# Two convolution layers with attention: where the second layer queues the next convolution's inputs and loads the third image

## The chip, the cores and the metric

The kernel runs on one core of a Trainium2 chip. The metric is the device time of one execution in microseconds (us); the time before is the median of three runs. One further execution was recorded by the hardware profiler, and all durations below come from it.

The engines are TensorE (PE in the profile, with its weight loads as PEld), VectorE (DVE), ScalarE (ACT), GpSimd (POOL) and SyncE (SP). Each works through its own queue in order. SyncE and ScalarE also issue DMAs from their queues: an issue that has to wait holds up what stands behind it.

## The reference, cut to what matters

Four images of 512 channels x 32 x 32 go through two layers. Each layer normalises its input by groups of 16 channels and adds its own result to the input. The first layer is a selective state-space scan and isn't touched. The second is, for each image:

```python
x_top    = conv1x1(x, w_top)                # 64 channels
x_center = conv1x1(x, w_center)             # 64 channels
x_bottom = conv3x3(x, w_bottom)             # 512 channels
sp  = softmax over all of (x_center^T x_top)   # 1024 x 1024, one softmax for the whole map
x   = x + (sp @ x_bottom)                   # reshaped as the image
out = conv3x3(x, w_out)
result = input + out                        # x above is the normalised input
```

All is float32.

## The kernel before

**The second layer's steps for image b.** The functions stand below with the profile's line numbers.

- norm loads the image (x1t, eight loads of 256 KB on ScalarE's queue, L1285), takes its statistics on VectorE (bn_stats, L1292, L1293), averages them by groups with a small matmul (pm_l, L1299), does the same for the deviations (pv_l, L1303), takes the root on ScalarE (L255, L256, with two table loads) and writes the normalised image xg (L1306). padded allots xg and clears its border with four memsets on POOL (L232 to L235).
- scores does the two 1 x 1 convolutions (pt, L1324), which ScalarE turns into center (L1329) and top (L1336), and the score map in 16 pieces (psc, L1345). ScalarE copies each piece into a tile st (L1349); eight such tiles, tag "st", hold the map. VectorE takes a maximum of each (mx, L1350), and ScalarE the exponential in place (L1359).
- conv3 named b0 to b3 is the 3 x 3 convolution with w_bottom, and conv3 named o0 to o3 the one with w_out. It works in transformed form: six row positions p, taken in the pairs (1, 2), (3, 4), (0, 5), times four column positions q, each a product of 4 x 4 chunks (m_b or m_o, L1494, 192 matmuls in a convolution). Its inputs are made by first_inputs or inputs: ScalarE and POOL make e and f (L1393, L1394), or POOL makes g, h, k, l; VectorE sums them into rr (L1396, L1397, L1460, L1469); and spread makes the four v from rr (L1374 to L1377). Each (p, q) needs 1 MB of transformed weights (uw_b, uw_o, L1490), which SyncE loads into three buffers of tag "u". ScalarE (L1502) and VectorE (L1510) take the products out of five PSUM buffers.
- attend multiplies the scores with the convolution's result, in eight steps k of 16 matmuls (pat, L1546), and adds each to xg on VectorE (L1559): I call this the attention's sum, and k = 7 the last one. The result of pat is in one of three PSUM buffers of tag "ps", which pt, psc, pm_l, pv_l and the final transposes use as well. For the first two images attend also does the remaining transforms of w_out, in pieces (wt, wr, wo, L1408 to L1437): VectorE computes them, SyncE stores them to u_o. wt, wo and the weights uw share the three "u" buffers, and rr and wr share the one of tag "rr".
- finish turns the result back with 32 transposes (po, L1586), adds it to the input loaded as o (L1576, L1591) and stores it (L1601, ScalarE's queue). last does it for the last image.

**The order.** The images go in pairs (a = 0 and a = 2). In a pair: b(a), attention of a with the norm of a + 1 inside, scores of a + 1, b(a + 1), inputs of o(a), attention of a + 1, o(a), finish, o(a + 1), finish. The norm of the third image (a + 2) is called inside o(a + 1), after its first inputs, through the argument mid.

**What sets the order on an engine.** The first layer's order is written out by a planner of its own. In the second layer, the framework fixes the order of each engine when the kernel is built, from the program's order, the dependencies, the free buffers and its estimates of durations. So an instruction can stand ahead of one that comes earlier in the program: ScalarE's e_o (L1393, inputs of o0) stands ahead of most copies of scores (L1349) in the trace, though scores is called first. Once built, an engine waits for the instruction that is at the head, whatever stands behind it.

**Buffers that matter.** Tag "v" has two buffers, for the v of the convolutions and for x1t. Tag "rt" has four, for e, f, g, h, k, l. The even images share one xg (pool cpool), the odd ones another (pool gp).

Of the kernel before, what the change touches and what calls it, by code (L numbers as in the profile page):

```python
# [8 lines left out]
F32 = mybir.dt.float32  # L9
# [6 lines left out]
P = 128  # L16
B, C, HH, WW = 4, 512, 32, 32
L = HH * WW
NCC = C // P
# [4 lines left out]
T = 512  # L24
# [145 lines left out]
def mamba_then_pab_kernel(  # L170
# [25 lines left out]
    nc = tc.nc  # L196
# [23 lines left out]
    brow = []  # L220
# [8 lines left out]
    def padded(b, pool, tag):  # L229

        xg = pool.tile([P, NCC, HH + 2, WW + 2], F32, tag=tag, name=f"xg_{b}")
        nc.gpsimd.memset(xg[:, :, 0, :], 0.0)  # L232
        nc.gpsimd.memset(xg[:, :, HH + 1, :], 0.0)
        nc.gpsimd.memset(xg[:, :, 1 : HH + 1, 0], 0.0)
        nc.gpsimd.memset(xg[:, :, 1 : HH + 1, WW + 1], 0.0)  # L235
        return xg
# [30 lines left out]
    image = {}  # L267
# [992 lines left out]
    with ExitStack() as l1:  # L1260
# [15 lines left out]
        NMC = L // P  # L1276
        HR = T // WW

        def norm(b):

            xg = padded(b, *((cpool, "image"), (gp, "xg"))[b % 2])
            t = xp.tile([P, NCC, L], F32, tag="v", name=f"x1t_{b}")
            for c in range(NCC):
                for h in range(NH):
                    nc.scalar.dma_start(  # L1285
                        t[:, c, h * T : (h + 1) * T], x1[b][h][c * P : (c + 1) * P, :]
                    )
            mv = spool.tile([P, NCC, 2], F32, tag="mv", name=f"mv_l1_{b}")
            for c in range(NCC):
                bs = spool.tile([P, NH, 6], F32, tag="bs", name=f"bs_l1_{b}_{c}")  # L1290
                for h in range(NH):
                    nc.vector.bn_stats(bs[:, h, :], t[:, c, h * T : (h + 1) * T])  # L1292
                nc.vector.bn_aggr(mv[:, c, :], bs)  # L1293
            mean, rstd, dev = (
                spool.tile([P, NCC], F32, tag=n, name=f"{n}_l1_{b}")
                for n in ("gmean", "grstd", "gdev")
            )
            p1 = ps.tile([P, T], F32, tag="ps", name=f"pm_l1_{b}")
            nc.tensor.matmul(p1[:, :NCC], gm_sb, mv[:, :, 0], start=True, stop=True)  # L1299
            deviation(p1, mv, mean, dev)  # L1300
            yield
            p2 = ps.tile([P, T], F32, tag="ps", name=f"pv_l1_{b}")
            nc.tensor.matmul(p2[:, :NCC], gm_sb, dev, start=True, stop=True)  # L1303
            rsqrt(rstd, p2[:, :NCC])
            for c in range(NCC):
                nc.vector.tensor_scalar(  # L1306
                    xg[:, c, 1 : HH + 1, 1 : WW + 1],
                    t[:, c].rearrange("p (h w) -> p h w", w=WW),
                    mean[:, c : c + 1], rstd[:, c : c + 1], ALU.subtract, ALU.mult,
                )  # L1310
            image[b] = xg

        def scores(b, xg):

# [121 lines left out]
            for q in (1, 2):  # L1436
                nc.sync.dma_start(dst[q], o[:, q - 1])  # L1437

        def conv3(name, xg, u, bias, first=None, late=None, mid=None):

# [32 lines left out]
            y = [None] * 4  # L1475
            for pair in PAIRS:
                if pair == (1, 2):
                    v = first or first_inputs(name, xg)
                    if mid:
                        mid()  # L1480
                else:
                    v = spread(name, pair[0], inputs(pair))
                ns = []
                for k, p in enumerate(pair):
                    m = {}
                    for q in (2, 1, 0, 3):
                        if late and (p, q) == (5, 3):
                            late(y)
                        w = fp.tile([P, NCC, C], F32, tag="u", name=f"uw_{name}_{p}_{q}", bufs=3)
                        nc.sync.dma_start(w, u[q][p])  # L1490
                        m[q] = pm.tile([P, C], F32, tag="m", name=f"m_{name}_{p}_{q}")
                        extra = (p, q) == (1, 1)
                        for c in range(NCC):
                            nc.tensor.matmul(  # L1494
                                m[q], v[:, q, k, c, :], w[:, c, :],
                                start=(c == 0), stop=(c == NCC - 1 and not extra),
                            )
                        if extra:
                            nc.tensor.matmul(m[q], ones[0:1, :], bias, start=False, stop=True)
                    al = ALPHA[p]  # L1500
                    e = lp.tile([P, C], F32, tag="e2", name=f"e2_{name}_{p}", bufs=2)
                    nc.scalar.activation(e, m[2], AF.Copy, scale=al / 2)  # L1502
                    n = lp.tile([P, 2, C], F32, tag="n", name=f"n_{name}_{p}", bufs=2)
                    for o, src, w, add, op in (
                        (n[:, 0], m[1], al / 2, e, ALU.add),
                        (n[:, 1], m[1], al / 2, e, ALU.subtract),
                        (n[:, 0], m[0], al, n[:, 0], ALU.add),
                        (n[:, 1], m[3], -al, n[:, 1], ALU.add),
                    ):
                        nc.vector.scalar_tensor_tensor(o, src, w, add, ALU.mult, op)  # L1510
                    ns.append(n)
                    if pair == (0, 5):
                        eng = nc.vector if late and k else nc.gpsimd
                        for c in range(2):
                            eng.tensor_add(y[3 * k][:, c], y[3 * k][:, c], n[:, c])
                if pair == (0, 5):
                    break

                a, d = (
                    lp.tile([P, 2, C], F32, tag="y", name=f"y_{name}_{pair[k]}", bufs=6)  # L1520
                    for k in range(2)
                )
                nc.gpsimd.tensor_add(a, ns[0], ns[1])
                nc.gpsimd.tensor_sub(d, ns[0], ns[1])
                if pair == (1, 2):
                    y[0], y[1] = a, d
                    continue

                y[2], y[3] = a, d
                f = [t.rearrange("p k o -> p (k o)") for t in y]  # L1530
                nc.gpsimd.tensor_add(y[0], y[0], y[2])
                nc.vector.scalar_tensor_tensor(f[1], f[3], 2.0, f[1], ALU.mult, ALU.add)
                nc.vector.scalar_tensor_tensor(f[2], f[2], 3.0, f[0], ALU.mult, ALU.add)
                nc.vector.scalar_tensor_tensor(f[3], f[3], 6.0, f[1], ALU.mult, ALU.add)
            return y

        def attend(b, xg, st, rp, xb, between, also):
# [4 lines left out]
            for k in range(NCC * NH):  # L1542
# [8 lines left out]
                if k == 0:  # L1551
# [4 lines left out]
                    for _ in between:  # L1556
                        pass
                img = xg[:, j, 1 + h * HR : 1 + (h + 1) * HR, 1 : WW + 1]
                nc.vector.scalar_tensor_tensor(  # L1559
                    img, pt.rearrange("p (h w) -> p h w", w=WW), rz, img,  # L1560
                    ALU.mult, ALU.add,
                )
                if also:
                    taps = piece_taps(also[k + 1]) if k + 1 < len(also) else None
                    piece(*ahead)
                    ahead = taps
                    if taps is None:
                        also = []

        dst = [out[b].rearrange("(c p) h w -> p c (h w)", p=P) for b in range(B)]  # L1570

# [23 lines left out]
        def finish(b, y):  # L1595

            for j in range(NCC):
                o = load_sum(b, j, fp, "f4")
                for rr in range(2):
                    turn_back(b, j, o, y, rr)  # L1600
                nc.scalar.dma_start(dst[b][:, j, :], o)  # L1601
# [11 lines left out]
                turn_back(b, j, o[j], y, 1)  # L1613
                (nc.scalar, nc.sync)[j % 2].dma_start(dst[b][:, j, :], o[j])

        def normed(b):
            for _ in norm(b):
                pass

        left = list(range(EARLY, NPC))  # L1620
        half = len(left) // 2
        st, rp = scores(0, image[0])
        for a in range(0, B, 2):
            for b in (a, a + 1):
                xb = conv3(f"b{b}", image[b], ub, brow[0])
                also = left[b * half : (b + 1) * half] if not a else []
                after, v = iter(()), None
                if b == a:
                    after = norm(b + 1)
                    next(after)  # L1630
                else:
                    v = first_inputs(f"o{a}", image[a])
                attend(b, image[b], st, rp, xb, after, also)
                if b == a:
                    st, rp = scores(b + 1, image[b + 1])
            finish(a, conv3(f"o{a}", image[a], uo, brow[1], v))
            if a + 2 == B:
                last(a + 1, image[a + 1], None)
                break
            y = conv3(f"o{a + 1}", image[a + 1], uo, brow[1], mid=lambda: normed(a + 2))  # L1640
            finish(a + 1, y)
            st, rp = scores(a + 2, image[a + 2])


# [55 lines left out]
```

## Time and profile before

| what | value |
|---|---|
| runs | 3053.99, 3060.0, 3060.22 us; median 3060.0 |
| profiled execution | 3048.93 us, span 3047.1 us |
| TensorE | busy 2742.4 us, 90% of the span, mean granted clock 0.972 |
| VectorE, ScalarE, GpSimd | busy 2402.3, 1842.4, 2022.1 us |
| DMA | 610.47 MB, 200 GB/s over the span |
| one weight load (1 MB) in the second layer | 4.8 us from issue to landing, median |
| x1t loads (256 KB) | 5.0 to 12.8 us from issue to landing, median 7.2 |
| o0 and o1, first matmul to first transpose | 2353.83 to 2439.15, and then to 2536.24 |

The chain of waits follows the work that ended last back to the start: TensorE has 45% of it, VectorE 23%, ScalarE 16%, DMA 6%. In a timeline a line gives start, duration, engine, line of the kernel, operation, output and inputs, count, and in brackets the idle time before it and what ended it. A granted clock of 1.0 is full speed.

### The profile page before, as it was taken

To read this page: it belongs to the slowest core of one execution; us is meant where nothing else is said; L and a number is where in the kernel's file an instruction comes from. 1 tells how busy PE (TensorE), PEld (TensorE's weight loads), DVE (VectorE), ACT (ScalarE), POOL (GpSimd) and SP (SyncE) were. 2 spreads that over 40 slices of the span, in tenths; PEclk is the share of its full clock that TensorE was granted. 3 is DMA by queue.
4 is the path that set the end of the run, shared out by engine and by line. 5 is a ranking of instruction groups with operands and counts; after the bars stand their busy time and mean duration, and the time that the engine had idled before them with its cause. 6 is when DMAs were issued, how large, how long until landed. Compare 5 with 4: busy or idle time off the path is not lost.

```text
span 3047.1 us, 35912 instructions
## 1 busy us (share of the span) xinstructions
PE 2742.4 (90%) x11512; PEld 1607.5 (53%) x11512; DVE 2402.3 (79%) x3171; ACT 1842.4 (60%) x3179; POOL 2022.1 (66%) x1047
## 2 busy tenths in 40 slices
PE   4789789999889999889999978799899999999998
PEld 2346556656666666556666655544344444444444
DVE  3469999989999989989999999976857575456164
ACT  4579989998789999789999888731110013030000
POOL 7899977899967889967889999843321331323132
PEclk8899999999999999989999999999999999999999
DMA  6766534567734567734566654748588896727497
GB/s 179 213 192 210 168 121 141 164 207 231 232 109 145 166 180 229 251 116 133 168 184 213 209 177 141 171 154 297 170 286 263 301 330 246 264 70 275 138 316 256
DMA packets 408947, 610.47 MB, mean 200 GB/s; under 512 B 46488, under 2 KB 245400, under 8 KB 384184
## 3 DMA queue, kind: packets, MB, share of 16 engines
q1 hardware_dynamic: 399952, 593.67, 61.8%
q10 hardware_dynamic: 8648, 14.26, 1.3%
q8 instruction: 92, 1.51, 0.2%
q14 instruction: 95, 0.78, 0.1%
q0 software_dynamic: 160, 0.26, 0.0%
HBM read 511.09 MB, written 96.99 MB: 200 GB/s over the span
## 4 chain that ended last, share of the span: by engine, by line
PE 45%; DVE 23%; ACT 16%; DMA 6%; issue 5%; POOL 4%; SPq 1%; ACTq 0%; DVEq 0%; POOLq 0%
PE m_o L1494 10%; PE m_b L1494 9%; DVE da L884 7%; PE y L913 5%; PE pz L394 4%; ACT sc L844 4%; PE pat L1546 4%; DVE u L884 3%; ACT da L832 3%; PE po L394 2%; PE u L870 2%; ACT u L832 2%; DVE dbx L884 2%; PE pxm L394 2%; PE psc L1345 2%
## 5 line engine op out<-in xcount | busy, mean ns | idle before, releaser
L906 POOL TENSOR_TENSOR da<-da,cbc 128x1024 f32<-128x1024 f32 x288 | 680.3, 2367 | 151.3 <-DVE carry_sb L889 63.6
L859 POOL TENSOR_TENSOR dbx<-dtx,bbc 128x1024 f32<-128x1024 f32 x224 | 529.6, 2368 | 59.1 <-PE y L913 34.9
L844 ACT ACTIVATE sc<-dtxt,bt_sb 128x256 f32<-128x256 f32 x1152 | 504.6, 497 | 46.2 <-PE u L870 46.0
L832 ACT ACTIVATE da<-dt,a_sb 128x512 f32<-128x512 f32 x576 | 395.0, 713 | 39.2 <-PE y L913 33.5
L884 DVE TENSOR_TENSOR_SCAN da<-da,carry_sb,u 128x512 f32<-128x512 f32 x288 | 356.0, 1262 | 27.3 <-PE u L870 22.0
L913 PE MATMUL y<-ident,da 128*128 128x128 f32 x2304 | 320.4, 283 | 58.3 <-POOL da L906 54.4
L870 PE MATMUL u<-ident,sc 128*128 128x128 f32 x2304 | 336.1, 278 | 35.3 <-DVE da L884 24.9
L913 PEld LDWEIGHTS y<-ident,da 128*128 128x128 f32 x2304 | 268.5, 145 | 161.2 <-POOL da L906 109.9
L884 DVE TENSOR_TENSOR_SCAN da<-da,u 128x512 f32<-128x512 f32 x288 | 348.8, 1211 | 3.9 <-PE u L870 3.6
L1494 PE MATMUL m_o<-uw_o,v_o 128*128 128x512 f32 x768 | 337.9, 599 | 4.4 <-DMA uw_o<-u_o 4.4
L1494 PE MATMUL m_b<-uw_b,v_b 128*128 128x512 f32 x768 | 333.4, 593 | 4.1 <-DMA uw_b<-u_b 4.1
L870 PEld LDWEIGHTS u<-ident,sc 128*128 128x128 f32 x2304 | 268.4, 143 | 112.2 <-DVE da L884 37.2
L832 ACT ACTIVATE u<-dt,a_sb 128x512 f32<-128x512 f32 x448 | 297.4, 681 | 36.8 <-DVE dbx L900 14.0
L394 PE MATMUL pxm<-xt,winc 128*128 128x345 f32 (+3 forms) x704 | 251.3, 499 | 29.3 <-DMA winc<-in_w_in_dram 16.5
L913 PE MATMUL y<-ident,dbx 128*128 128x128 f32 x1792 | 252.9, 279 | 23.7 <-POOL dbx L906 14.4
L913 PEld LDWEIGHTS y<-ident,dbx 128*128 128x128 f32 x1792 | 207.5, 143 | 99.7 <-issue 32.2
L394 PE MATMUL pz<-xt,winc 128*128 128x512 f32 x512 | 242.1, 600 | 11.7 <-ACT sz L707 2.1
L1494 PEld LDWEIGHTS m_o<-uw_o,v_o 128*128 128x128 f32 x768 | 145.9, 192 | 188.0 <-issue 180.7
L1494 PEld LDWEIGHTS m_b<-uw_b,v_b 128*128 128x128 f32 x768 | 145.0, 190 | 188.9 <-issue 179.5
L906 POOL TENSOR_TENSOR dbx<-dbx,cbc 128x1024 f32<-128x1024 f32 x96 | 226.7, 2362 | 26.0 <-DVE carry_sb L889 17.5
L1546 PE MATMUL pat<-y_b,st 128*128 128x512 f32 x512 | 221.6, 593 | 1.6 <-DVE rz L1555 1.5
L394 PEld LDWEIGHTS pxm<-xt,winc 128*128 128x128 f32 x704 | 132.0, 198 | 117.1 <-issue 62.1
(235 smaller groups left out, 4331.5 us busy)
## 6 DMA issues: line engine op xcount, KB each, us to landing
cbc<-bcd SPq DMA_DIRECT2D x512, 256.0 KB, 3.6
uw_b<-u_b SPq DMA_DIRECT2D x96, 1024.0 KB, 4.8
uw_o<-u_o SPq DMA_DIRECT2D x96, 1024.0 KB, 4.8
bbc<-bcd SPq DMA_DIRECT2D x224, 256.0 KB, 3.6
u_b<-work SPq DMA_DIRECT2D x192, 128.0 KB, 2.8
winc<-in_w_in_dram SPq DMA_DIRECT2D x72, 256.0 KB, 3.8
szd<-sz SPq DMA_DIRECT2D x32, 512.0 KB, 3.5
szl<-szd SPq DMA_DIRECT2D x32, 512.0 KB, 5.0
```

What stands on the lines that cost most here:

```text
L394: lambda k=k, lhs=lhs, rhs=rhs: nc.tensor.matmul(p()[:, at : at + cols], lhs(), rhs(), start=(k == 0), stop=(k == n - 1)),
L832: nc.scalar.activation(t, dt()[:, j], AF.Exp, scale=a_sb[:, at : at + 1])
L844: nc.scalar.activation(sc()[:, k], dtxt()[:, k], AF.Copy, scale=bt[:, at, s : s + 1])
L859: lambda: nc.gpsimd.tensor_mul(hc(), dtx(), b_bc().to_broadcast([P, 2, T])),
L870: nc.tensor.transpose(u()[:, k * P : (k + 1) * P], sc()[:, k, j, :], ident)
L884: nc.vector.tensor_tensor_scan(ht, *((hc()[:, j], u()) if on_act else (u(), hc()[:, j])), carry_sb[:, j, s : s + 1] if h else 0.0, ALU.mul ...
L906: lambda: nc.gpsimd.tensor_mul(hc(), hc(), c_bc().to_broadcast([P, 2, T])),
L913: nc.tensor.matmul(y[j]()[:, k, :], hc()[:, j, k * P : (k + 1) * P], ident, start=(s == 0 and k == 0), stop=(s == NS - 1 and k == NK - 1), ...
L1345: nc.tensor.matmul(pt, top[:, m * P : (m + 1) * P], center[:, h * T : (h + 1) * T], start=True, stop=True,)
L1494: nc.tensor.matmul(m[q], v[:, q, k, c, :], w[:, c, :], start=(c == 0), stop=(c == NCC - 1 and not extra),)
L1546: nc.tensor.matmul(pt, st[m][:, 2 * P * j + h : 2 * P * (j + 1) : 2], xb[m // 2][:, m % 2, :], start=(m == 0), stop=(m == NMC - 1),)
```

## The change

It has two parts.

First, conv3 gets an argument behind in place of mid. For the second image of a pair it is the last attention sum of the first image (attend now returns it), and everything that first_inputs puts on that sum's engine, VectorE, gets an issue edge to it: it has to stand behind that sum in VectorE's queue. It is an order, not a semaphore. For the first image of a pair, behind is None.

Second, the third image's norm leaves o1. norm now pauses twice: after the statistics, and after the deviations. With spare=True it loads the image into four tiles of tag "st" in place of one of tag "v". For image 2 the loads and statistics are called ahead of o0, the mean and deviations after o0's matmuls, and the root and the normalised image after finish of image 0 and ahead of o1. padded is now called just ahead of the normalised image, for the second and fourth image too; apart from that their norm keeps its order.

```diff
@@ -1276,25 +1276,29 @@
         NMC = L // P
         HR = T // WW
 
-        def norm(b):
-
-            xg = padded(b, *((cpool, "image"), (gp, "xg"))[b % 2])
-            t = xp.tile([P, NCC, L], F32, tag="v", name=f"x1t_{b}")
-            for c in range(NCC):
+        def norm(b, spare=False):
+
+            if spare:
+                ts = [xp.tile([P, L], F32, tag="st", name=f"x1t_{b}_{c}", bufs=NMC) for c in range(NCC)]
+            else:
+                t = xp.tile([P, NCC, L], F32, tag="v", name=f"x1t_{b}")
+                ts = [t[:, c] for c in range(NCC)]
+            for c, t in enumerate(ts):
                 for h in range(NH):
                     nc.scalar.dma_start(
-                        t[:, c, h * T : (h + 1) * T], x1[b][h][c * P : (c + 1) * P, :]
+                        t[:, h * T : (h + 1) * T], x1[b][h][c * P : (c + 1) * P, :]
                     )
             mv = spool.tile([P, NCC, 2], F32, tag="mv", name=f"mv_l1_{b}")
-            for c in range(NCC):
+            for c, t in enumerate(ts):
                 bs = spool.tile([P, NH, 6], F32, tag="bs", name=f"bs_l1_{b}_{c}")
                 for h in range(NH):
-                    nc.vector.bn_stats(bs[:, h, :], t[:, c, h * T : (h + 1) * T])
+                    nc.vector.bn_stats(bs[:, h, :], t[:, h * T : (h + 1) * T])
                 nc.vector.bn_aggr(mv[:, c, :], bs)
             mean, rstd, dev = (
                 spool.tile([P, NCC], F32, tag=n, name=f"{n}_l1_{b}")
                 for n in ("gmean", "grstd", "gdev")
             )
+            yield
             p1 = ps.tile([P, T], F32, tag="ps", name=f"pm_l1_{b}")
             nc.tensor.matmul(p1[:, :NCC], gm_sb, mv[:, :, 0], start=True, stop=True)
             deviation(p1, mv, mean, dev)
@@ -1302,13 +1306,13 @@
             p2 = ps.tile([P, T], F32, tag="ps", name=f"pv_l1_{b}")
             nc.tensor.matmul(p2[:, :NCC], gm_sb, dev, start=True, stop=True)
             rsqrt(rstd, p2[:, :NCC])
-            for c in range(NCC):
+            xg = image[b] = padded(b, *((cpool, "image"), (gp, "xg"))[b % 2])
+            for c, t in enumerate(ts):
                 nc.vector.tensor_scalar(
                     xg[:, c, 1 : HH + 1, 1 : WW + 1],
-                    t[:, c].rearrange("p (h w) -> p h w", w=WW),
+                    t.rearrange("p (h w) -> p h w", w=WW),
                     mean[:, c : c + 1], rstd[:, c : c + 1], ALU.subtract, ALU.mult,
                 )
-            image[b] = xg
 
         def scores(b, xg):
 
@@ -1436,7 +1440,7 @@
             for q in (1, 2):
                 nc.sync.dma_start(dst[q], o[:, q - 1])
 
-        def conv3(name, xg, u, bias, first=None, late=None, mid=None):
+        def conv3(name, xg, u, bias, first=None, late=None, behind=None):
 
 
 
@@ -1475,9 +1479,8 @@
             y = [None] * 4
             for pair in PAIRS:
                 if pair == (1, 2):
-                    v = first or first_inputs(name, xg)
-                    if mid:
-                        mid()
+                    with tc.issue_after(behind.ins) if behind else ExitStack():
+                        v = first or first_inputs(name, xg)
                 else:
                     v = spread(name, pair[0], inputs(pair))
                 ns = []
@@ -1556,7 +1559,7 @@
                     for _ in between:
                         pass
                 img = xg[:, j, 1 + h * HR : 1 + (h + 1) * HR, 1 : WW + 1]
-                nc.vector.scalar_tensor_tensor(
+                ins = nc.vector.scalar_tensor_tensor(
                     img, pt.rearrange("p (h w) -> p h w", w=WW), rz, img,
                     ALU.mult, ALU.add,
                 )
@@ -1566,6 +1569,7 @@
                     ahead = taps
                     if taps is None:
                         also = []
+            return ins
 
         dst = [out[b].rearrange("(c p) h w -> p c (h w)", p=P) for b in range(B)]
 
@@ -1613,32 +1617,35 @@
                 turn_back(b, j, o[j], y, 1)
                 (nc.scalar, nc.sync)[j % 2].dma_start(dst[b][:, j, :], o[j])
 
-        def normed(b):
-            for _ in norm(b):
-                pass
-
         left = list(range(EARLY, NPC))
         half = len(left) // 2
         st, rp = scores(0, image[0])
         for a in range(0, B, 2):
+            ins = None
             for b in (a, a + 1):
-                xb = conv3(f"b{b}", image[b], ub, brow[0])
+                xb = conv3(f"b{b}", image[b], ub, brow[0], behind=ins)
                 also = left[b * half : (b + 1) * half] if not a else []
                 after, v = iter(()), None
                 if b == a:
                     after = norm(b + 1)
                     next(after)
+                    next(after)
                 else:
                     v = first_inputs(f"o{a}", image[a])
-                attend(b, image[b], st, rp, xb, after, also)
+                ins = attend(b, image[b], st, rp, xb, after, also)
                 if b == a:
                     st, rp = scores(b + 1, image[b + 1])
-            finish(a, conv3(f"o{a}", image[a], uo, brow[1], v))
+            if a + 2 < B:
+                after = norm(a + 2, True)
+                next(after)
+            y = conv3(f"o{a}", image[a], uo, brow[1], v)
+            next(after, None)
+            finish(a, y)
             if a + 2 == B:
                 last(a + 1, image[a + 1], None)
                 break
-            y = conv3(f"o{a + 1}", image[a + 1], uo, brow[1], mid=lambda: normed(a + 2))
-            finish(a + 1, y)
+            next(after, None)
+            finish(a + 1, conv3(f"o{a + 1}", image[a + 1], uo, brow[1]))
             st, rp = scores(a + 2, image[a + 2])
 
 
```

## The prediction

> **What bounds the kernel now.** I read the page first, then the timeline of the second layer engine by engine, then busy time by stretches. The page's chain of waits is led by TensorE, and the second layer (from about 2000 us on) is all m_b, m_o, pat and psc matmuls, so a change here is worth what it takes from PE's idle time and from stretches at a reduced clock. TensorE's timeline has two bad places. The first is the step from the first image's attention to the second image's first convolution:
>
> ```profile
> 2170.91 3.61 PE L1324 MATMUL pt<-xg,wt_sb 128*128 128x512 f32 x8
> 2176.76 3.71 PE L1324 MATMUL pt<-xg,wt_sb 128*128 128x512 f32 x8 [2.24 <-DVE xg L1559]
> 2180.31 1.88 PE L1494 MATMUL m_b<-uw_b,v_b 128*128 128x512 f32 x4
> 2188.05 5.36 PE L1345 MATMUL psc<-center,top 128*128 128x512 f32 x6 [5.86 <-DVE xg L1559]
> 2198.03 14.08 PE L1345 MATMUL psc<-center,top 128*128 128x512 f32 x26 [4.62 <-ACT st L1349]
> ```
>
> The bracket is idle time and its releaser. The columns of the next view are one stretch: length, busy time and count of PE, PEld, DVE, ACT, POOL, then clock and DMA. It sets this step beside the same step for images three and four:
>
> ```profile
> 2170.91:2211.95 41.04, 28.31 (x53) 11.39 (x52) 33.41 (x28) 14.44 (x27) 16.52 (x6) 0.83 0.34 109
> 2702.11:2724.45 22.34, 22.34 (x53) 9.84 (x52) 8.97 (x8) 14.74 (x27) 9.55 (x4) 1.00 0.00 1
> ```
>
> The same 53 matmuls take 18.7 us longer in the first pair. VectorE's and ScalarE's timelines say why:
>
> ```profile
> 2175.96 0.75 DVE L1559 SCALAR_TENSOR_TENSOR xg<-pat,rz,xg 128x512 f32<-128x512 f32 x1
> 2176.62 1.28 DVE L1397 TENSOR_TENSOR rr_b<-e_b,f_b 128x1088 f32<-128x1088 f32 x1
> 2177.93 1.23 DVE L1374 TENSOR_TENSOR v_b<-rr_b 128x1024 f32<-128x1024 f32 x1
> 2179.08 3.55 DVE L1375 TENSOR_TENSOR v_b<-rr_b 128x1024 f32<-128x1024 f32 x1
> 2182.55 3.55 DVE L1376 TENSOR_TENSOR v_b<-rr_b 128x1024 f32<-128x1024 f32 x1
> 2187.16 0.74 DVE L1559 SCALAR_TENSOR_TENSOR xg<-pat,rz,xg 128x512 f32<-128x512 f32 x1
> 2196.39 1.11 ACT L1393 ACTIVATE e_o<-xg 128x1088 f32<-128x1088 f32 x1 [13.94 <-DVE rr_b L1469]
> ```
>
> The last attention sum (L1559, 2187.16) empties a PSUM buffer that psc needs; its matmuls ended near 2171, but VectorE first ran the second image's convolution inputs. Then ScalarE sat at e_o, whose buffer the later rr_b (L1469) frees, with the copies of psc behind it. The second bad place is inside the second image's last convolution:
>
> ```profile
> 2460.72 0.56 PE L1299 MATMUL pm_l<-mv_l,gm_sb 128*128 128x4 f32 x2 [6.05 <-DVE mv_l L1293]
> 2461.14 5.35 PE L1494 MATMUL m_o<-uw_o,v_o 128*128 128x512 f32 x6
> 2353.83 8.70 PE L1494 MATMUL m_o<-uw_o,v_o 128*128 128x512 f32 x16 [3.05 <-DMA uw_o<-u_o]
> ```
>
> The third image's mean waits 6.05 us for its statistics, and the next six matmuls go at half pace. The last line is the start of the first image's last convolution, where the change adds loads.
>
> **What the Trainium skill says.** "TensorE: Matmul & The Clock Gate", What's actually happening: about 3.4 us of idleness halves the array's clock, and about as much work restores it. The trace agrees: after the 5.86 and 6.05 us gaps a matmul takes 0.86 us instead of 0.43, and even the 3.05 us gap costs (16 matmuls in 8.70 us, not 6.9); 1.53 us at 2122 cost nothing. "SBUF — State Buffer", Who interferes with whom: a Vector instruction with two SBUF inputs contends with a GpSimd one that reads SBUF. Here L1375 and L1376 take 3.55 us beside POOL's l_b and k_b, 1.2 us without. "DMA: Bandwidth & Descriptors", Issuing engines are not separate DMA queues: loads on ScalarE's queue run on the same 16 DMA engines as SyncE's. Agreed: when the fourth image's x1t came beside b2's weights (2617 to 2636), PE waited 1.35 + 0.15 us for uw_b.
>
> **Part 1, the issue edge behind the attention's last sum.** It adds no instruction; it holds six VectorE instructions (two rr sums, L1396 and L1397, and four v, L1374 to L1377) behind the last L1559, for the second convolution of each pair, b1 and b3. ScalarE's and POOL's share of the same inputs (L1393, L1394) is not held.
>
> First pair. The last wo piece before it ends at 2173.5; both remaining L1559 (0.7 each) then end at 2174.9. PE: second pt 2174.4 to 2178.0; ScalarE's center and top take 1.95, so psc can start at 2180.1. Its 32 matmuls take 13.9 (as at 2710), to 2194.2, with four m_b in the 2 us before psc. Their input: 2174.9 + two rr sums 2.5 + L1374 1.2 = 2178.6, in time. The other three v take 3.5 + 3.5 + 1.2 beside POOL, to 2186.8; PE wants them at 2194.2. So the step ends at 2194.2, not 2211.95: **17.7 gained**. What is late next: nothing but the weights. The fourth uw_b waits behind o loads on SyncE in either version (1.30 us PE wait at 2221.95, which I leave standing). All of 2288 to 2353, where SyncE and the weight pieces lead, hangs from PE's release of u buffers at 2288 and moves with it.
>
> ScalarE's e_o must not stay ahead of the 16 score copies. L1469 now follows the whole chain: 0.75 + 2.5 + 4.6 + 2.5 + 4.6 + 1.2 = 16.2 of VectorE work after pat's end, with eight reductions (1.22 each) of higher rank arriving from 11 us on: 26 us. The copies end some 23 us after pat. An order that is worked out with such costs, as the one shown appears to be (there L1469 ends just when the copies start, and e_o stands just ahead of them), puts e_o behind all or nearly all of them. The three ps buffers cover two copies.
>
> Second pair. No idle time is to be gained there. v now starts at 2703.1, first use 2706.8, the rest by 2715, needed at 2724.45: **0**, hidden by psc. If that cover goes, see the rivals.
>
> **Part 2, the third image's norm.** Removed from the second image's last convolution: that stretch (first po 2439.15 to the next 2536.24) is 97.09. Its work is 192 matmuls x 0.4307 = 82.7, bias 1.05, transposes 3.8, pm and pv 0.6: 88.1. So 9.0 is lost: 6.05 idle, 2.6 for six slow matmuls. The step from o2 to o3, without such a norm, loses 0.38 + 0.94; that from o1 to b2 nothing. I leave 0.7 and count **8.3 gained**. x1t also no longer holds one of two v buffers.
>
> Moved: 8 loads of 256 KB on ScalarE's queue (0.35 us each; the queue has only evacuations near then), eight bn_stats of 0.69 and four aggregates of 0.2 on VectorE (6.3 us; it idles 7.2, 2.3 and 2.7 us at 2356 to 2370), two small matmuls, two table loads of 1.28 on ScalarE (idle over 13 us between evacuations), four L1306 (2.98) and POOL's four memsets (1.2, POOL idle): **0**, hidden, the mean now being ready long before PE comes to it. The change adds two waits. The loads wait on ScalarE's queue for attention to leave the score tiles (by 2350.8); behind them stand e_o and f_o for the next convolution and the first evacuation of m_o (2359), for which PE has five buffers. The bn_stats wait on VectorE for the loads; behind them stand v_o of the second pair of rows and the last L1559, which PE needs only at 2382. For the second and fourth image only the border memsets come later, and VectorE's L1306 after them: POOL is idle from 2116.8 to 2126.4, so 0.
>
> The DMA is not free. Four score tiles come free one by one over the last 7 us of attention, 2344 to 2350, so 2.1 MB start just before uw_o (2347.64, 6.14 us to landing), and SyncE's last u_o stores are still under way. From below 0 (PE waits there anyway), the row of b2 gives 1.5, from above all 2.1 MB at 420 GB/s, the rate while x1t landed there, ahead of uw_o: 5.0. I take **2.5 lost**, since the start has no weights in hand. A gain is excluded: no byte is taken away.
>
> **The sum.** 17.7 + 8.3 - 2.5 = 23.5. The profiled execution had a span of 3047.1 and took 3048.9, so 3025.4 on its scale. It was 0.36% faster than the median, 3060.0; against that, **3036.5**.
>
> **The rivals.** A: as above, 3036.5; own range 3026 to 3046 (2.5 to 5.0 or 0, the v chain late by some us, the profile's lower base).
> B: e_o lands among the copies, say after the twelfth, in both pairs. e_o ends 22.3 us after pat in the second pair, 25.3 in the first; four copies (3.4) and a cold clock (3.4) follow, against an end at 23.7: second pair 5.4 lost, first 8.4 of the gain. 23.5 - 13.8 = 9.7: 3050. For: POOL stretches the chain beyond any plan without it. Against: the reductions in between.
> C, **slower**: e_o and f_o stand ahead of the first copy in both pairs. They stand ahead of center even now in the third image's attention, harmlessly, the chain having run early (2665). Then psc starts at 22.3 and ends at 22.3 + 13.9 + 3.4 = 39.6, against 22.3 now: 17.3 lost in the second pair, the first keeps its 41: -17.3 + 5.8 = -11.5: 3071.5. It turns from gain to loss with about six copies ahead of e_o: each one more takes 0.86 off the loss of either pair.
> D: the loads delay o0's start to a cold and starved one: 10 lost instead of 2.5: 3044. For: 16 slow matmuls there already. Against: from 2340 to 2350 the DMA engines were busy for 0.74 only.
> E: nothing changes: L1559 was late for the pieces' DMAs, which stay, and pm_l waits elsewhere: 3060. Against: both late sums end together at 2174.9.
>
> **Chances.** About 0.2% (6 us) is what a measurement of this kernel tells from no change. A 0.54, D 0.12, B 0.12 (half of it faster by over 6 us, half within), E 0.06, C 0.16. Faster 0.54 + 0.12 + 0.06 = 0.72; same 0.12; slower 0.16. The range runs from 3024 to 3062: it leaves out C and a little below A.
>
> **What would show it.** Right: the last two L1559 ahead of rr_b L1396; psc without gaps, that stretch near 23.5; pm_l without idle time; clock 1.0 in both. Wrong: ACT waiting at e_o with copies behind it, a longer step in the second pair, or more than 5.5 us idle ahead of the first m_o.

## The result, and the profile after

The changed kernel took 3029.8 us (median of five, 3028.91 to 3036.43), the kernel before 3053.99 (median of five, 3049.64 to 3060.22): ratio 0.993, 95% interval 0.9911 to 0.995. Three of these five runs before are those of the table above; the two others took 3049.64 and 3051.13 us. In a second comparison, with 3050.63 us before (median of eleven) and 3032.43 after (median of six), the ratio was 0.9946 (0.9932 to 0.996). So the change makes the kernel faster by 0.5 to 0.7%, 24.2 us in the medians of the first comparison and 18.2 in those of the second; 23.5 us (0.8%) were forecast. The profiled execution has a span of 3027.8 us against 3047.1.

TensorE's timeline after. The columns are start, duration, engine, line, operation, count, and in brackets the idle time before and its releaser. Line numbers are 3 or 4 higher than before: pt is L1328, psc L1349, m_b and m_o L1497, the attention's sum L1562, e_o L1397.

```profile
2175.33 7.22 PE L1328 MATMUL pt<-xg,wt_sb 128*128 128x512 f32 x16
2183.49 1.96 PE L1497 MATMUL m_b<-uw_b,v_b 128*128 128x512 f32 x4 [0.93 <-DMA uw_b<-u_b]
2185.28 13.90 PE L1349 MATMUL psc<-center,top 128*128 128x512 f32 x32
...
2231.41 51.77 PE L1497 MATMUL m_b<-uw_b,v_b 128*128 128x512 f32 x120 [1.71 <-ACT e_b L1505]
...
2343.00 9.56 PE L1497 MATMUL m_o<-uw_o,v_o 128*128 128x512 f32 x16 [4.67 <-DMA uw_o<-u_o]
...
2429.19 0.28 PE L1303 MATMUL pm_l<-mv_l,gm_sb 128*128 128x4 f32 x2
...
2737.68 51.77 PE L1497 MATMUL m_b<-uw_b,v_b 128*128 128x512 f32 x120 [0.82 <-ACT e_b L1505]
```

psc now runs through without a gap, and pm_l waits for nothing. o0 starts after 4.67 us of waiting instead of 3.05. Two waits for e_b are new, in b1 and in b3. By stretches (length, then busy time and count of PE, PEld, DVE, ACT, POOL, then clock and DMA), the step after the first attention and o1 with its turn before it:

```profile
2175.33:2199.02 23.69, 22.76 (x54) 9.69 (x53) 23.44 (x20) 12.66 (x25) 6.98 (x2) 1.00 0.56 189
2429.33:2519.03 89.70, 88.34 (x232) 39.87 (x231) 57.01 (x70) 8.62 (x12) 35.92 (x15) 1.00 0.92 328
```

Before, these two took 41.04 and 97.09 us; the granted clock is 1.00 in both now. VectorE and ScalarE in the step:

```profile
2178.05 1.40 DVE L1562 SCALAR_TENSOR_TENSOR xg<-pat,rz,xg 128x512 f32<-128x512 f32 x2
2179.37 1.28 DVE L1400 TENSOR_TENSOR rr_b<-e_b,f_b 128x1088 f32<-128x1088 f32 x1
2206.30 1.28 DVE L1473 SCALAR_TENSOR_TENSOR rr_b<-l_b,g_b 128x1088 f32<-128x1088 f32 x1
2207.61 1.11 ACT L1397 ACTIVATE e_o<-xg 128x1088 f32<-128x1088 f32 x1 [7.80 <-DVE rr_b L1473]
```

Both late sums now stand ahead of rr_b, and e_o comes after the last of the 16 score copies (2199.22).

I follow the second layer by stretches of TensorE's timeline, cut where the work changes. This keeps the first layer out of the comparison: its order is the same in both kernels, yet the first attention starts at 2113.74 us before and at 2118.18 after, and between 2110 and 2124 over the ten profiles of this study. The names of columns are those of the experiments below; again is the changed kernel's second profile. The stretches that are left out agree within 0.2 us, but for 0.5 us in one of inputs ahead.

| stretch, us | before | after | again | edge only | norm only | inputs behind copies | loads later | reduce first | both | inputs ahead |
|---|---|---|---|---|---|---|---|---|---|---|
| step: first pt to first m_b behind psc | 41.04 | 23.69 | 23.66 | 23.30 | 39.88 | 33.51 | 23.47 | 23.64 | 23.66 | 40.05 |
| b1 from there | 83.51 | 83.99 | 83.46 | 83.79 | 81.94 | 81.93 | 83.64 | 81.93 | 81.93 | 74.68 |
| attention 2 to the first m_o | 58.37 | 59.99 | 60.64 | 58.41 | 60.71 | 58.27 | 57.74 | 59.87 | 58.51 | 59.95 |
| o0 to its first po | 85.32 | 86.33 | 86.20 | 85.45 | 86.20 | 83.76 | 86.32 | 85.58 | 84.97 | 86.07 |
| o1, first po to the next | 97.09 | 89.70 | 89.83 | 96.20 | 89.40 | 97.43 | 89.75 | 90.04 | 89.72 | 89.53 |
| b2 from there | 110.20 | 109.21 | 110.17 | 109.87 | 110.43 | 109.70 | 110.27 | 109.96 | 110.34 | 114.17 |
| step of the second pair | 22.34 | 22.34 | 22.34 | 22.34 | 22.34 | 22.35 | 22.34 | 22.34 | 22.34 | 36.20 |
| b3 from there | 81.93 | 83.02 | 83.01 | 83.06 | 81.93 | 81.93 | 83.14 | 81.93 | 81.94 | 75.92 |
| o3 | 86.12 | 84.02 | 84.75 | 85.16 | 84.06 | 84.01 | 89.01 | 84.86 | 84.13 | 84.01 |
| first attention to the end of o3 | 917.57 | 893.93 | 895.69 | 899.15 | 908.59 | 904.56 | 897.36 | 891.80 | 889.20 | 912.78 |

### The profile page after: what moved, and what is told of

Same layout as the page of the kernel before. It is cut to its first block, busy times and chain, and to the rows that moved or that the text cites. A ratio compares the mean times of both kernels' runs of the same rounds, so it can differ in the third digit from the quotient of the medians.

```text
span 3027.8 us, 35925 instructions
## 1 busy us (share of the span) xinstructions
PE 2738.9 (90%) x11512; PEld 1609.8 (53%) x11512; DVE 2390.2 (79%) x3171; ACT 1842.8 (61%) x3179; POOL 2023.5 (67%) x1047
## 5 line engine op out<-in xcount | busy, mean ns | idle before, releaser
L1497 PE MATMUL m_o<-uw_o,v_o 128*128 128x512 f32 x768 | 336.1, 597 | 5.7 <-DMA uw_o<-u_o 5.7
L1497 PE MATMUL m_b<-uw_b,v_b 128*128 128x512 f32 x768 | 333.6, 593 | 5.5 <-ACT e_b L1505 2.5
L870 PEld LDWEIGHTS u<-ident,sc 128*128 128x128 f32 x2304 | 270.9, 144 | 110.4 <-DVE da L884 38.0
L832 ACT ACTIVATE u<-dt,a_sb 128x512 f32<-128x512 f32 x448 | 297.5, 681 | 35.6 <-DVE dbx L900 13.9
L1497 PEld LDWEIGHTS m_b<-uw_b,v_b 128*128 128x128 f32 x768 | 144.8, 190 | 190.8 <-issue 179.1
L1497 PEld LDWEIGHTS m_o<-uw_o,v_o 128*128 128x128 f32 x768 | 145.4, 191 | 188.0 <-issue 179.2
```

The costliest lines, as they stand in the source:

```text
L832: nc.scalar.activation(t, dt()[:, j], AF.Exp, scale=a_sb[:, at : at + 1])
L870: nc.tensor.transpose(u()[:, k * P : (k + 1) * P], sc()[:, k, j, :], ident)
L1497: nc.tensor.matmul(m[q], v[:, q, k, c, :], w[:, c, :], start=(c == 0), stop=(c == NCC - 1 and not extra),)
```

## The experiments

**Edge only.** The kernel before, with part 1 alone: conv3 gets behind as in the change, and keeps mid and the norm in o1.

> The kernel before with part 1 alone (the issue edge); the third image's norm stays in o1. Theory: the parts are independent. The step from the second image's first pt to the first m_b behind the scores falls from 41.04 to 23.7 us, b1 and b3 grow by 0.5 and 1.1 as after the whole change (GpSimd's all-reduce is late), o0's start stays at a 3 us wait, o1 stays at 97.1. Whole: -16 us, ratio 0.995. Rival (the norm's move is needed for part of it, through the buffers that it frees): the step stays above 27 us.

Measured: 3038.96 us against 3050.24, ratio 0.9962 (0.9953 to 0.9972). The step is 23.30, b3 83.06, o0's start has its 3.08 us wait, o1 96.20 with 6.23 us ahead of pm_l. Each stretch came as the theory says; the rival falls. In this run too e_o comes after all the score copies (2206.05 against 2197.55 for the last), so the edge alone moves it there. The whole time moved by 0.38%, less than the 0.5% expected. A likely reason, not shown, is the profile of before that I added up from: it has waits of its own in b1 and o3 that other runs lack (below), and its step of 41.04 us takes 39.88 in the next run, where the same instructions stand in it.

**Norm only.** The changed kernel without the edge:

```diff
-                xb = conv3(f"b{b}", image[b], ub, brow[0], behind=ins)
+                xb = conv3(f"b{b}", image[b], ub, brow[0])
```

> The changed kernel without the issue edge: part 2 alone. Theory: the step stays at 41 us, o1 falls from 97.1 to 89.7, o0's start and its first 16 matmuls cost 2.6 more. Whole: -5 us, ratio 0.9985, hardly to be told from no change. Rival (the loads beside the first weights cost as much as o1 gives): 0 or slower.

Measured: 3048.72 us, ratio 0.9994 (0.9985 to 1.0004). The step is 39.88, o1 89.40, attention 2 and o0 together 146.91 against 143.69 before. So the stretches are as expected (7.7 gained in o1, 3.2 lost at o0's start), while the whole time can't be told from no change: for the rival, which forecast 0 or slower, only the stretches speak against it. The whole times of the two parts add up to 0.44%, against 0.54 and 0.7% for the change. b1 takes 81.94 here and b3 81.93: without the edge there is no wait for e_b.

**Inputs behind copies.** The kernel before; only ScalarE's e and f of o0 and o2 are put behind the last score copy:

```diff
-                    nc.scalar.copy(t[:, h * T : (h + 1) * T], pt)
+                    copied = nc.scalar.copy(t[:, h * T : (h + 1) * T], pt)
...
-                    v = first_inputs(f"o{a}", image[a])
+                    with tc.issue_after(copied.ins):
+                        v = first_inputs(f"o{a}", image[a])
```

> The kernel before, with ScalarE's e_o and f_o alone put behind the last score copy; VectorE's order is untouched. Theory of two waits in a row: the wait of psc for the last attention sum stays (5.9 us idle), the 4.6 us wait behind e_o goes with the slow clock after it; the step is 34 to 35 us instead of 41.0. Rival (the late attention sum alone makes the step long, ScalarE only shows it): 40 to 41 us.

Measured: the step is 33.51, of which the whole of psc is this line of TensorE's timeline:

```profile
2194.45 16.61 PE L1345 MATMUL psc<-center,top 128*128 128x512 f32 x32 [5.86 <-DVE xg L1559]
```

The wait for the attention's sum is there as before, 5.86 us, and the one behind e_o is gone. So the 17.35 us are two waits in a row: 7.5 behind e_o with its slow clock, the rest behind the late sums (2.16 us of waiting in pt, 5.86 in psc, and the slower matmuls after it). The edge on VectorE removes both: edge only shows that e_o moves with it. That the framework moves e_o because its buffer comes free later is inferred, since no run shows how the order is worked out. (The whole time, 3042.38 us, is that of a single run and says little by itself.)

**Inputs ahead.** The changed kernel with the opposite order forced, as rival C had it:

```diff
                     v = first_inputs(f"o{a}", image[a])
+                    for e in made[-2:]:
+                        tc.add_manual_dep(
+                            copies[0].ins, e.ins.name,
+                            mybir.DependencyInfo(mybir.DependencyClass.NoSync, mybir.DependencyReason.DATA),
+                            reason="ahead",
+                        )
```

copies holds ScalarE's score copies in order, made the e and f. The edge holds the first copy of the program; one other copy still came ahead of e_o in each pair (at 2179.39 in the first).

> The changed kernel with an order edge that keeps ScalarE's copy of the first score piece (m = 0, h = 0) behind e_o and f_o, in both pairs: nearly the order of rival C. Rival C's price: psc can only go on once e_o is through, 22 to 25 us after the last pat, so the step takes about 40 us in both pairs, b1 and b3 stay at 83 to 84, and about 34 us are lost against the changed kernel. The other view: an order that is built knowing of the delay lets TensorE do products of b1 and b3 (five buffers, 17 us) ahead of psc, so that the step grows but b1 and b3 shrink by most of it; under 8 us are lost in all, each pair (step and b) staying under 112.

```profile
2177.47 3.68 PE L1350 MATMUL psc<-center,top 128*128 128x512 f32 x8
2180.99 5.31 PE L1498 MATMUL m_b<-uw_b,v_b 128*128 128x512 f32 x12
2186.23 1.12 PE L1503 MATMUL m_b<-brow_b,ones 1*128 1x512 f32 x2
2187.28 1.12 PE L1498 MATMUL m_b<-uw_b,v_b 128*128 128x512 f32 x2
2194.65 13.18 PE L1350 MATMUL psc<-center,top 128*128 128x512 f32 x24 [6.24 <-ACT st L1354]
```

Neither expectation holds. The first pair's step and b1 take 114.73 together, 7.6 more than the repeat of the changed kernel, the second pair's 112.12, 6.8 more: 14.4 lost, not 34. The order that was built fills part of the wait with products of b1 (14 of their instructions and the bias stand between the score pieces), and 6.24 us stay (4.50 in the second pair). The 4 us by which b2 is longer are waits for weights (2.41 and 1.44) of which I don't know whether they belong to the edit. So rival C's mechanism is real, but its price in the prediction was more than twice too high: it took the order of TensorE as given. With 14.4 lost from a forecast of 23.5 gained, it would still have ended faster than before; the single run took 3040.83 us, against 3048.27 for a single run of the kernel before beside it.

**Loads later.** The changed kernel with the third image's loads behind ScalarE's first evacuation in o0 (its first copy of a product out of PSUM):

```diff
-                    nc.scalar.activation(e, m[2], AF.Copy, scale=al / 2)
+                    ev = nc.scalar.activation(e, m[2], AF.Copy, scale=al / 2)
+                    if mid and p == 1:
+                        with tc.issue_after(ev.ins):
+                            mid()
...
-                next(after)
-            y = conv3(f"o{a}", image[a], uo, brow[1], v)
+            y = conv3(
+                f"o{a}", image[a], uo, brow[1], v,
+                mid=(lambda: next(after)) if a + 2 < B else None,
+            )
```

> The changed kernel with the third image's eight loads put behind ScalarE's first evacuation in o0. Theory: the loads cost o0 its start. The wait ahead of the first m_o goes back from 4.7 to about 3 us and the first 16 matmuls from 9.56 to about 8.7, 2.6 us in all; later in o0 up to 1.5 us of waits for weights come instead. Rival (the start varies by itself, or SyncE's stores set it): the wait stays at 4 to 5 us.

```profile
2342.25 8.83 PE L1497 MATMUL m_o<-uw_o,v_o 128*128 128x512 f32 x16 [2.42 <-DMA uw_o<-u_o]
...
2363.12 3.24 PE L1497 MATMUL m_o<-uw_o,v_o 128*128 128x512 f32 x7 [0.48 <-DMA uw_o<-u_o]
```

The wait ahead of o0 falls from 4.67 (5.30 in the repeat) to 2.42, and 0.48 comes later. Attention 2 and o0 together take 144.06 instead of 146.32 and 146.84: 2.3 to 2.8 us, as expected. All ten profiles agree: these two stretches take 142.0 to 144.1 us in the five without loads ahead of o0 (before, edge only, inputs behind copies, loads later, both) and 145.5 to 146.9 in the five with them. The loads are what o0's start pays for. (The run's 3035.19 us holds an o3 of 89.01 with a 2.01 us wait for weights, where the edit changes nothing.)

**Reduce first.** The changed kernel with GpSimd's part of o0's and o2's inputs behind the all-reduce of the score maxima (red, returned by scores):

```diff
-                    v = first_inputs(f"o{a}", image[a])
+                    with tc.issue_after(red.ins):
+                        v = first_inputs(f"o{a}", image[a])
...
-                    v = spread(name, pair[0], inputs(pair))
+                    with tc.issue_after(red.ins) if red and pair == (3, 4) else ExitStack():
+                        r = inputs(pair)
+                    v = spread(name, pair[0], r)
```

This goes after the new waits for e_b. GpSimd in the kernel before, then GpSimd and VectorE in the changed kernel:

```profile
2214.32 0.38 POOL L1355 PARTITION_ALL_REDUCE ma<-mp  x1 [7.20 <-DVE mp L1353]
...
2208.80 3.27 POOL L1398 TENSOR_TENSOR e_o<-e_o,xg 128x1088 f32<-128x1088 f32 x1 [19.82 <-ACT e_o L1397]
2212.03 2.52 POOL L1460 TENSOR_TENSOR g_o<-xg 128x1088 f32<-128x1088 f32 x1
2221.06 0.38 POOL L1359 PARTITION_ALL_REDUCE ma<-mp  x1 [6.50 <-issue]
2221.47 0.15 DVE L1360 TENSOR_SCALAR ma<-ma 128x1 f32<-128x1 f32 x1 [9.70 <-POOL ma L1359]
```

Before, GpSimd had ended the inputs of o0 (e_o, g_o, h_o, f_o) 7.2 us ahead of the all-reduce, which followed the maxima (mp) at once. In the changed kernel the maxima are there at 2209.97, while e_o and g_o run until 2214.55.

> The changed kernel with GpSimd's part of o0's and o2's inputs put behind the all-reduce of the score maxima. Theory: in the changed kernel the all-reduce starts 6.5 us after g_o ends, which is GpSimd's change to it, and that lies in the open only because g_o and e_o run right ahead of it; with GpSimd idle before, it is over before the maxima are there. VectorE's wait for ma falls from 9.7 to under 1 us, and PE's waits of 1.71 us in b1 and 0.82 us in b3 for e_b go. Rival (the reduction itself takes 6 us, or ScalarE's exponentials hold e_b anyway): PE's waits stay above 0.8 us each or move.

GpSimd in this run:

```profile
2213.35 0.38 POOL L1359 PARTITION_ALL_REDUCE ma<-mp  x1 [21.18 <-DVE mp L1357]
2222.32 2.28 POOL L1398 TENSOR_TENSOR e_o<-e_o,xg 128x1088 f32<-128x1088 f32 x1 [8.60 <-ACT st L1363]
```

The all-reduce now follows the maxima at once (releaser mp). b1 takes 81.93 and b3 81.93, both without a wait: 2.1 and 1.1 us less than in the changed kernel. The theory holds. In the changed kernel e_o and g_o stand ahead of the all-reduce on GpSimd; it starts 6.5 us after them (the last section has what stands between); VectorE's ma, ScalarE's eight exponentials and e_b behind them follow late; and TensorE runs out of its five product buffers. (The single run took 3030.85 us, against 3050.63 before, median of eleven.)

**Both, and the change again.** Loads later and reduce first together, beside the changed kernel on the same chip.

> The changed kernel with both: loads behind o0's first evacuation, and the all-reduce ahead of GpSimd's inputs. Theory: the sum of the two, 2.6 + 2.5 less some waits for weights: 3 to 5 us under the changed kernel, ratio to before 0.9915. Rival: the waits come back elsewhere, and it equals the changed kernel.

> The changed kernel once more, on the chip of the run with both, for a direct comparison: ratio to before 0.993. Steps as before within 1 us: 23.7 us for the step after the first attention, 4 to 5 us of waiting ahead of the first m_o, PE's waits for e_b in b1 and b3, o1 at 89 to 91. If the start of o0 or the waits differ by over 1.5 us between the two executions, they are chance and no cost of the change.

Measured: both 3026.75 us, ratio 0.9919 (0.9906 to 0.9931); the changed kernel 3032.43, ratio 0.9946 (0.9932 to 0.996), where 0.993 was expected. The stretches of the repeat are as they were within 0.8 us, except b2 by 0.96. Both is 5.7 us under the change, somewhat more than expected; by the stretches 3.4 are at o0's start, 1.5 in b1 and 1.1 in b3. It is the fastest kernel here; its interval lies just below that of the change on its chip.

## Why the prediction was right, and where its terms were off

The time lay in the range, faster by about what was forecast, and each main term came from the place named. The forecast of 3036.5 us was counted from 3060.0; the median before is 3053.99 in the comparison, which is 6.0 of the 6.7 us by which the measured 3029.8 lies below it. Against the profile of before:

| term of the sum | predicted | measured |
|---|---|---|
| the step, part 1 | -17.7 | -17.35 (again -17.38) |
| b1, b3 behind it | 0, 0 | +0.48, +1.09 |
| o0's start | +2.5 | +2.63 |
| o1 | -8.3 | -7.39 |
| b2, o3 | 0, 0 | -0.99, -2.10 |
| sum | -23.5 | -23.64 |

**The step** was right down to its parts. The sums end 4.1 us after pt starts (4.0 predicted) and psc starts at 9.95 (9.2 predicted). Ahead of it stands a wait of 0.93 us for uw_b, which is more than the difference. psc takes 13.9, as predicted.

**e_o's place.** The argument was that L1469 falls behind enough work to leave e_o behind all the copies. It did: e_o comes 8.4 us after the last copy starts. The sum behind it was too short: VectorE gives up e_o's buffer some 32 us after pat's end, not 26, which only helped. "Inputs ahead" shows the point mattered: near the other order each pair loses 7.

**"What is late next: nothing but the weights", and the second pair's 0.** These failed. The same delay that moved e_o behind the copies put e_o and g_o in front of the all-reduce on GpSimd. I counted ScalarE's side of moving these inputs and not GpSimd's queue. The price is the e_b wait in both pairs: b1 83.5 to 84.0 with the edge and GpSimd's order as it is, 81.9 without the edge (norm only, inputs behind copies) or with the reduction first, b3 83.0 against 81.9, about 3 us in all. Against the profile of before, only 0.5 of it shows in b1, because that profile has 1.30 us of waiting for uw_b there. I had left that standing as fixed; it was absent in both other runs without the edge, so I take it for chance.

**o0's start** was a bracket from 0 to 5.0, and 2.5 was picked in its middle: that it came to 2.63 is in part luck, the cause is not. It was 3.2 in norm only, and went with the loads moved. Of it, 1.62 are waiting; the rest is a slower start.

**o1** gave 7.4, not 8.3: the wait for pm_l and the six slow matmuls went, but 0.51, 0.52 (weights) and 0.34 (a transpose) came, 1.4 and not 0.7.

**The sum is better than its terms.** b2 and o3 give 3.1 us that belong to nothing in the change: over the runs, with and without it, o3 takes 84.0 to 89.0 and b2 (inputs ahead apart) 109.2 to 110.4. Without this and the 1.30 of b1, the terms are -17.35 + 1.78 + 2.63 - 7.39 + 1.09 = -19.24, or 0.63%, between the two measured ratios. That the profiles agree with 23.5 so closely is luck; the forecast was too large by some 4 us, 3 of them the e_b waits.

Of the rivals, B (e_o among the copies) and E (nothing) didn't happen; D's mechanism is what o0's start pays, at 2.6 and not 10; C didn't happen, and its price was too high.

## What to carry to other kernels

Where an engine that nobody calls the bound holds a buffer, ask first what stands ahead of the releasing instruction in its queue: one issue edge on VectorE took 17 us off TensorE. When such an edge delays a chain, follow everything fed by that chain into each queue that it enters, the least busy engine's too: here GpSimd's inputs slipped in front of a reduction and cost 3 us of the gain. To judge terms of a few us, cut the timeline into stretches and compare several runs of each, since single waits for weights came and went with 1 to 5 us in a stretch that no edit touched.

## What the runs showed of the hardware that was not expected

GpSimd's all-reduce takes 0.38 us (the first of a run 3.41), but right behind a tensor operation on the same engine it starts 6.0 to 7.5 us after it (2214.55 to 2221.06 in the first pair of the changed kernel, releaser "issue"; 6.03 in the repeat, 7.34 in the second pair, 7.47 in that of loads later), and the next tensor operation comes 7.5 to 9.4 us after it (2228.90; 2222.32 in reduce first; 9.4 in both). With GpSimd idle beforehand the first delay is hidden. The list of the instructions of this line in the changed kernel has one more kind, which the timeline leaves out:

```profile
L1359 POOLq MODIFY_POOL_CONFIG  x8: 1/6/11, 2035.5 to 2720.2; - x8
L1359 POOL PARTITION_ALL_REDUCE ma<-mp x4: 378/378/3407, 2046.2 to 2727.3; - x4
```

So two changes of GpSimd's configuration stand ahead of each of the four all-reduces, and in the trace two more behind it. The delay runs from them: they come at 2214.75, right behind g_o, in the changed kernel, and at 2192.37, 21 us ahead of the all-reduce, in reduce first. What they do in that time no run shows.

How long TensorE may idle before it goes on slowly is not one number near 3 us. The 16 first matmuls of o0 took 8.83 us after 2.42 us of waiting (loads later) and 8.70 after 3.05 (before), but 7.13 after 2.94 (inputs behind copies) and after 3.18 in the run with both:

```profile
2341.30 7.13 PE L1499 MATMUL m_o<-uw_o,v_o 128*128 128x512 f32 x16 [3.18 <-DMA uw_o<-u_o]
```

It is the clock: over the first 2 us of these matmuls the granted clock was 0.50 before and 1.00 in both; in loads later it was 0.69, and 0.50 over the 2 us after that. The prediction counted its 3.05 us gap as agreeing with the length of idleness that it cites; the gap is shorter than that, and 2.42 us was enough here.

What decides seems to be where the wait lies. From 2060 us on, the granted clock in all ten traces changes only at steps of 3.413 us. In the step that ended last before the clock fell to 0.50 at o0's start, TensorE was idle for 60 to 95% (eight profiles); in the two where it stayed at 1.00 (inputs behind copies, both), no step was idle for more than 53%. In loads later the 2.42 us lay in one step, from 2339.59 to 2343.00; in both the 3.18 us lay across two. It is not a full rule: two falls in inputs ahead follow steps that were idle for 37 and 38%. So whether a wait of 2.4 to 3.2 us costs nothing or about 1.7 us seems to hang on its place among these steps, which no edit here sets.
